# Two graph-attention layers: the second layer as (A x1) W with x1 as the stationary operand, e_i and e_j by VectorE multiply-accumulate, and its outputs in later slots

One core of one Trainium2 chip. The metric is the device time of the whole program in microseconds (us), the median over its runs; lower is better. A run is called fast when it is not over 1.5% above the fastest run of the same kernel. All runs quoted here were correct against the reference.

## The reference

128 batches of 128 nodes with 512 features, all in float32. Layer 0 is attention with 8 heads under the adjacency mask; layer 1 is a graph attention with one head. Cut to layer 1 and the frame:

```python
def _L1_gnn_ref(h, adj, W, a):
    Wh = jnp.matmul(h, W)                       # W: 512 x 512
    a1, a2 = a[:Fout, 0], a[Fout:, 0]
    e_i = jnp.einsum('bnf,f->bn', Wh, a1)
    e_j = jnp.einsum('bnf,f->bn', Wh, a2)
    e = jax.nn.leaky_relu(e_i[:, :, None] + e_j[:, None, :], negative_slope=0.2)
    e = jnp.where(adj == 0, MASK_VAL, e)
    attention = jax.nn.softmax(e, axis=2)       # A: 128 x 128 per batch
    return jax.nn.elu(jnp.matmul(attention, Wh))

x = _layernorm(x + _L0_gnn_ref(x, adj, ...))    # this is x1
x = _layernorm(x + _L1_gnn_ref(x, adj, W, a))
```

## The kernel before

Batches go in groups of four, and the loop runs over slots, one per batch. In each slot stand one batch's attention weights, a fourth of the next group's projections (slot 0: transposes of x; then pqT; pkT; pv), the attention output of the batch before, and a share of layer 1 of the group before. The Tile framework orders the instructions of each engine and picks the buffers. All small PSUM tiles come from one pool of four banks (`ps`). Layer 1 and the schedule, with cuts:

```python
def x1_transposes(g, i):                                   # 4 transposes per batch, then a VectorE copy
    transposed(X1T[g][:, :, i, :], X1[g][:, i, :], ...)

def graph_weights(g):                                      # wa = W @ a1, W @ a2
    for c in range(NC):                                    # pj: e_j on all partitions, 4 products x 512 columns
        nc.tensor.matmul(pj, wa2_bc[:, c, :], X1T[g][:, c, :, :], ...)
    for i in range(G):                                     # pi: e_i, 16 products x 1 column
        for c in range(NC):
            nc.tensor.matmul(pi[:, i:i + 1], X1T[g][:, c, i, :], wa[:, 0, c:c + 1], ...)
    ...                                                    # e, leaky relu, mask, softmax without its division

def graph_values(g):                                       # pw = x1 W: 16 products x 512 columns per group
    for i in range(G):
        for c in range(NC):
            nc.tensor.matmul(p, X1T[g][:, c, i, :], w_sb[:, c, :], ...)
        nc.scalar.copy(WH[g, i], p)

def graph_output(g, i):                                    # ph = A (x1 W): 1 product x 512 columns per batch
    nc.tensor.matmul(p, ATT_T[g][:, i, :], WH.pop((g, i)), start=True, stop=True)
    nc.scalar.activation(t, p, AF.Exp, scale=r)            # elu: ScalarE, GpSimd, VectorE in turn; p is held until y
    nc.gpsimd.tensor_scalar(t, t, 1.0, -1.0, op0=ALU.min, op1=ALU.add)
    nc.vector.scalar_tensor_tensor(y, p, r, t, op0=ALU.mult, op1=ALU.max)
    ...                                                    # + x1, layer norm, store

def layer1(g, step):
    if step == 1:   graph_weights(g); graph_values(g)
    elif step == 2: graph_weights_t(g); graph_output(g, 0); graph_output(g, 1)
    elif step == 3: graph_output(g, 2); graph_output(g, 3)
```

Of the kernel before, what the change touches and what calls it, by code (L numbers as in the profile page):

```python
# [11 lines left out]
ALU = mybir.AluOpType  # L12
AX = mybir.AxisListType

N_BATCH = 128


@with_exitstack
def tile_two_graph_layers(ctx: ExitStack, tc: tile.TileContext, x, adj, wq, bq, wk, bk, wv, bv, wo, bo, w, a, out,
                          n_batch=N_BATCH):  # L20
    """Multi-head graph attention, then single-head graph attention, each with residual and layer norm.

    A batch is 128 nodes, one partition block. Batches are taken in groups of four so that the
    projections stream 512 nodes. All matrix products are float32.
    """
    nc = tc.nc
    P = 128
    D = x.shape[2]
# [1 line left out]
    H = 8  # L30
    DH = D // H
    G = 4
    NG = n_batch // G
    NEG = -1.0e9
    EPS = 1e-5
    ALPHA = 0.2
# [6 lines left out]
    ps_big = ctx.enter_context(tc.tile_pool(name="ps_big", bufs=2, space=bass.MemoryType.PSUM))  # L43
    ps = ctx.enter_context(tc.tile_pool(name="ps", bufs=4, space=bass.MemoryType.PSUM))

    # state of the groups and batches in flight
    X, ADJ, MASK, XT, QT, KT, V, PR, X1, X1T, WH, ATT, RI, ATT_T = ({} for _ in range(14))

    def load(g):
        X[g] = three.tile([P, G, D], F32, tag="x", name=f"x_{g}")  # L50
# [4 lines left out]

    load(0)

# [1 line left out]
    ident = const.tile([P, P], F32, tag="ident", name="ident")  # L59
    make_identity(nc, ident)  # L60
    half = const.tile([P, 1], F32, tag="half", name="half")
# [24 lines left out]
    bv_bc = on_all_partitions(bv, 0, "bv")  # L86
    bo_bc = on_all_partitions(bo, 0, "bo")

    # the queries carry the 1/sqrt(head dim) of the logits
    qscale = 1.0 / DH ** 0.5  # L90
    bqs = const.tile([P, NC], F32, tag="bqs", name="bqs")
    nc.vector.tensor_scalar_mul(bqs, bq_sb, qscale)

    # W @ a1 and W @ a2, so that e_i and e_j come from the layer's input
    wa = const.tile([P, 2, NC], F32, tag="wa", name="wa")
    for s in range(2):
        a_bc = two.tile([P, D], F32, tag="o", name=f"a_bc{s}")
        nc.gpsimd.dma_start(a_bc, bass.AP(tensor=a.tensor, offset=a.offset + s * D, ap=[[0, P], [1, D]]))
        for c in range(NC):
            scr = two.tile([P, D], F32, tag="y", name=f"wa_scr{s}_{c}")  # L100
            nc.vector.scalar_tensor_tensor(scr, w_sb[:, c, :], 1.0, a_bc, op0=ALU.mult, op1=ALU.mult,
                                           accum_out=wa[:, s, c:c + 1])
    wa2_bc = const.tile([P, NC, P], F32, tag="wa2_bc", name="wa2_bc")
    nc.vector.tensor_copy(wa2_bc, wa[:, 1, :].unsqueeze(2).to_broadcast([P, NC, P]))

    def transposed(dst, src, name):
        """dst[p, c, n] = src[n, c * 128 + p]"""
        p = ps.tile([P, NC, P], F32, tag="ps", name=name)
        for c in range(NC):
            nc.tensor.transpose(p[:, c, :], src[:, c * P:(c + 1) * P], ident)  # L110
        nc.vector.tensor_copy(dst, p)  # L111
# [8 lines left out]
        nc.gpsimd.tensor_tensor(rstd, rstd, half, op=ALU.pow)  # L120
        nc.vector.tensor_scalar(dst, src, mv[:, 0:1], rstd, op0=ALU.subtract, op1=ALU.mult)  # L121

# [1 line left out]
    def x_transposes(g):  # L124
        MASK[g] = two.tile([P, G, P], I32, tag="mask", name=f"mask_{g}")
        nc.vector.tensor_scalar(MASK[g], ADJ[g], 0.0, None, op0=ALU.is_gt)
# [19 lines left out]
            nc.vector.tensor_add(V[g, i], p, bv_bc)  # L146

    def attention_weights(g, i):
        """Softmax over the unmasked keys; heads stand as (h % 2, h // 2)."""
        s = ps_big.tile([P, 2, H // 2, P], F32, tag="big", name=f"s_{g}_{i}")  # L150
        for hp in range(H // 2):
            for j in range(2):
                r = slice(j * DH, (j + 1) * DH)
                nc.tensor.matmul(s[:, j, hp, :], QT[g][r, hp, i, :], KT[g][r, hp, i, :], start=True, stop=True)  # L154
        pr = two.tile([P, H, P], F32, tag="pr", name=f"pr_{g}_{i}")
        nc.gpsimd.memset(pr, NEG)  # L156
        nc.vector.copy_predicated(pr, MASK[g][:, i, :].unsqueeze(1).to_broadcast([P, H, P]),  # L157
                                  s.rearrange("p j h k -> p (j h) k"))
        nmax = small.tile([P, H], F32, tag="nmax", name=f"nmax_{g}_{i}")
        nc.vector.tensor_reduce(nmax, pr, AX.X, ALU.max, negate=True)  # L160
        tot = small.tile([P, H], F32, tag="tot", name=f"tot_{g}_{i}")
        for h in range(H):
            nc.scalar.activation(pr[:, h, :], pr[:, h, :], AF.Exp, bias=nmax[:, h:h + 1], scale=1.0,  # L163
                                 accum_out=tot[:, h:h + 1])
        nc.vector.reciprocal(tot, tot)
        nc.gpsimd.tensor_tensor(pr, pr, tot.unsqueeze(2).to_broadcast([P, H, P]), op=ALU.mult)  # L166
        PR[g, i] = pr

    def attention_output(g, i):
        pr = PR.pop((g, i))  # L170
        pT = ps_big.tile([P, 2, H // 2, P], F32, tag="big", name=f"ppT_{g}_{i}")
        for j in range(2):
            for hp in range(H // 2):
                nc.tensor.transpose(pT[:, j, hp, :], pr[:, j * (H // 2) + hp, :], ident)  # L174
        prT = two.tile([P, 2, H // 2, P], F32, tag="prT", name=f"prT_{g}_{i}")
        nc.scalar.copy(prT, pT)  # L176
        v = V.pop((g, i))
        po = ps.tile([P, H // 2, P], F32, tag="ps", name=f"po_{g}_{i}")
        for hp in range(H // 2):
            for j in range(2):  # L180
                h = 2 * hp + j
                nc.tensor.matmul(po[j * DH:(j + 1) * DH, hp, :], v[:, h * DH:(h + 1) * DH], prT[:, j, hp, :],  # L182
                                 start=True, stop=True)
        oT = two.tile([P, H // 2, P], F32, tag="oT", name=f"oT_{g}_{i}")
        nc.scalar.copy(oT, po)  # L185
        py = ps.tile([P, D], F32, tag="ps", name=f"py_{g}_{i}")
        for c in range(NC):
            nc.tensor.matmul(py, oT[:, c, :], wo_sb[:, c, :], start=(c == 0), stop=(c == NC - 1))  # L188
        o = two.tile([P, D], F32, tag="o", name=f"o_{g}_{i}")
        nc.vector.tensor_add(o, py, bo_bc)  # L190
        nc.vector.scalar_tensor_tensor(o, o, 0.0, X[g][:, i, :], op0=ALU.max, op1=ALU.add)
        if i == 0:
            X1[g] = two.tile([P, G, D], F32, tag="x1", name=f"x1_{g}")
            X1T[g] = one.tile([P, NC, G, P], F32, tag="x1T", name=f"x1T_{g}")
        layer_norm(X1[g][:, i, :], o, f"0_{g}_{i}")

    def x1_transposes(g, i):
        transposed(X1T[g][:, :, i, :], X1[g][:, i, :], f"px1T_{g}_{i}")

# [1 line left out]
    def graph_weights(g):  # L201
        pj = ps.tile([P, G, P], F32, tag="ps", name=f"pj_{g}")
        for c in range(NC):
            nc.tensor.matmul(pj, wa2_bc[:, c, :], X1T[g][:, c, :, :], start=(c == 0), stop=(c == NC - 1))  # L204
        pi = ps.tile([P, G], F32, tag="ps", name=f"pi_{g}")
        for i in range(G):
            for c in range(NC):
                nc.tensor.matmul(pi[:, i:i + 1], X1T[g][:, c, i, :], wa[:, 0, c:c + 1],  # L208
                                 start=(c == 0), stop=(c == NC - 1))
        ei = small.tile([P, G], F32, tag="ei", name=f"ei_{g}")  # L210
        nc.vector.tensor_copy(ei, pi)
        e = one.tile([P, G, P], F32, tag="e", name=f"e_{g}")
        nc.vector.tensor_tensor(e, pj, ei.unsqueeze(2).to_broadcast([P, G, P]), op=ALU.add)
        nc.vector.scalar_tensor_tensor(e, e, ALPHA, e, op0=ALU.mult, op1=ALU.max)
        at = two.tile([P, G, P], F32, tag="at", name=f"at_{g}")
        nc.gpsimd.memset(at, NEG)
# [8 lines left out]
        nc.vector.reciprocal(RI[g], tot)  # L225
        ATT[g] = at

    def graph_values(g):
        for i in range(G):
            p = ps.tile([P, D], F32, tag="ps", name=f"pw_{g}_{i}")  # L230
            for c in range(NC):
                nc.tensor.matmul(p, X1T[g][:, c, i, :], w_sb[:, c, :], start=(c == 0), stop=(c == NC - 1))  # L232
            WH[g, i] = two.tile([P, D], F32, tag="wh", name=f"wh_{g}_{i}", bufs=4)
            nc.scalar.copy(WH[g, i], p)

    def graph_weights_t(g):
        p = ps.tile([P, G, P], F32, tag="ps", name=f"pat_{g}")
        for i in range(G):
# [1 line left out]
        ATT_T[g] = two.tile([P, G, P], F32, tag="attT", name=f"attT_{g}")  # L240
        nc.vector.tensor_copy(ATT_T[g], p)

    def graph_output(g, i):
        p = ps.tile([P, D], F32, tag="ps", name=f"ph_{g}_{i}")
        nc.tensor.matmul(p, ATT_T[g][:, i, :], WH.pop((g, i)), start=True, stop=True)  # L245
        r = RI[g][:, i:i + 1]
        # elu(h) = max(h, min(exp(h), 1) - 1), with the softmax's division in h
        t = two.tile([P, D], F32, tag="t", name=f"t_{g}_{i}")
        nc.scalar.activation(t, p, AF.Exp, scale=r)  # L249
        nc.gpsimd.tensor_scalar(t, t, 1.0, -1.0, op0=ALU.min, op1=ALU.add)  # L250
# [3 lines left out]
        layer_norm(y, y, f"1_{g}_{i}")  # L254
        nc.sync.dma_start(out[g * G + i], y)

# [1 line left out]
    # Per slot one batch's attention weights, the output of the batch before it, the layer-1 input of the batch  # L258
    # before that, and a share of the next group's projections and of the previous group's layer 1.
    def projections(g, step):  # L260
        if not 0 <= g < NG:
            return
# [11 lines left out]
    def layer1(g, step):  # L274
        if not 0 <= g < NG:
            return
        if step == 1:
            graph_weights(g)
            graph_values(g)
        elif step == 2:  # L280
            graph_weights_t(g)
            graph_output(g, 0)
            graph_output(g, 1)
        elif step == 3:
            graph_output(g, 2)
            graph_output(g, 3)

    for step in range(G):
        projections(0, step)
    slots = [(g, i) for g in range(NG) for i in range(G)]  # L290
    for t in range(len(slots) + G):
        g, i = divmod(t, G)
        if t < len(slots):
            attention_weights(g, i)
        projections(g + 1, i)
        if 0 <= t - 2 < len(slots):
            x1_transposes(*slots[t - 2])
        if 0 <= t - 1 < len(slots):
            attention_output(*slots[t - 1])
        layer1(g - 1, i)  # L300


# [22 lines left out]
```

## Time and profile before

| | before |
|---|---|
| time | 3663.18 us, median of 4 runs, 3655.35 to 3669.01 |
| TensorE busy | 3328.2 us, 91% of the span |
| VectorE, ScalarE, GpSimd busy | 36, 27, 27% |
| mean granted TensorE clock | 0.935 of full speed |
| one group of four batches | 112.6 us |

The lines are in the prediction. Two readings carry over. The group repeats 32 times, so 1 us per group is about 0.9% of the time. And the clock is part of the cost: the clock records hold only full and half, so 0.935 over 3661 us is (1 - 0.935) x 2 x 3661 = 476 us at half clock.

### The profile page before, as it was taken

The page shows a single profiled execution, that of the slowest core. Times are in us where ns is not written, and L with a number is a line of the kernel's source. Part 1 is how long each engine was busy: PE and PEld are TensorE (multiplying, and loading weights), DVE is VectorE, ACT ScalarE, POOL GpSimd, SP SyncE. Part 2 cuts the span into 40 slices and gives each one's busy share as a digit, 9 for nine tenths or more (in the row PEclk, how much of TensorE's full clock was granted, in tenths as well). Part 3 has the DMA queues.
Part 4 walks back from the last instruction along what each step waited for, and adds up shares of the span by engine and source line. Part 5 has one row for each costly group of instructions (what it writes and reads, how often), then busy time and mean ns, then how long its engine had stood idle before and what let it go on. Part 6 is the DMA issues. An engine that isn't in the chain of part 4 may idle for free.

```text
span 3661.1 us, 33875 instructions
## 1 busy us (share of the span) xinstructions
PE 3328.2 (91%) x12928; PEld 1762.8 (48%) x12928; DVE 1334.7 (36%) x2194; ACT 995.6 (27%) x3073; POOL 989.1 (27%) x1069
## 2 busy tenths in 40 slices
PE   7999999999999999999999999999999999999995
PEld 3545444455444454444544445544445444454452
DVE  2343334333343333343333433334333334333343
ACT  1222322222222223222232222222222322223231
POOL 1132223222233222232222322223322223222233
PEclk9999999999999999999999999999999999999997
DMA  3000000000000000000000000000000000000000
GB/s 112 12 26 9 20 26 26 23 12 24 21 26 24 15 21 21 26 24 26 9 21 26 27 23 12 23 21 26 24 15 21 21 26 24 26 9 20 12 12 23
DMA packets 55411, 83.98 MB, mean 23 GB/s; under 512 B 3280, under 2 KB 19664, under 8 KB 55248
## 3 DMA queue, kind: packets, MB, share of 16 engines
q1 hardware_dynamic: 52224, 75.51, 5.9%
q10 hardware_dynamic: 2640, 5.24, 0.4%
q8 instruction: 102, 1.67, 0.2%
q0 software_dynamic: 384, 1.05, 0.1%
q14 instruction: 61, 0.50, 0.0%
HBM read 48.24 MB, written 33.55 MB: 22 GB/s over the span
## 4 chain that ended last, share of the span: by engine, by line
PE 83%; POOL 6%; ACT 3%; DVE 3%; issue 3%; DMA 1%; ACTq 0%; SPq 0%; POOLq 0%; DVEq 0%
PE py L188 14%; PE pw L232 14%; PE pqT L136 12%; PE pkT L136 12%; PE pv L144 12%; PE po L182 4%; PE pj L204 3%; PE pi L208 3%; PE ppT L174 3%; POOL t L250 3%; PE ph L245 2%; POOL y L253 2%; PE px1T L110 2%; ACT prT L176 2%; PE s L154 1%
## 5 line engine op out<-in xcount | busy, mean ns | idle before, releaser
L188 PE MATMUL py<-wo,oT 128*128 128x512 f32 x1024 | 534.5, 670 | 26.6 <-ACT oT L185 23.6
L163 ACT ACTIVATE pr<-pr,nmax 128x128 f32<-128x128 f32 x1024 | 396.1, 388 | 386.4 <-DVE nmax L160 383.4
L232 PE MATMUL pw<-w,x1T 128*128 128x512 f32 x1024 | 500.9, 652 | 0.0
L111 DVE COPY x1T<-px1T 128x512 f32<-128x512 f32 x128 | 87.8, 686 | 1049.8 <-PE px1T L110 1049.6
L156 POOL MEMSET pr<- 128x1024 f32 x128 | 121.8, 952 | 1269.4 <-PE ppT L174 1269.4
L136 PE MATMUL pqT<-xT,wq 128*128 128x512 f32 x1024 | 446.4, 594 | 16.3 <-DVE xT L111 16.3
L136 PE MATMUL pkT<-xT,wk 128*128 128x512 f32 x1024 | 444.8, 592 | 0.0
L144 PE MATMUL pv<-wv,xT 128*128 128x512 f32 x1024 | 444.7, 592 | 0.0
L166 POOL TENSOR_TENSOR pr<-pr,tot 128x1024 f32<-128x1024 f32 x128 | 243.6, 1903 | 454.4 <-DVE mv L118 245.2
L232 PEld LDWEIGHTS pw<-w,x1T 128*128 128x128 f32 x1024 | 210.9, 209 | 264.4 <-issue 264.4
L188 PEld LDWEIGHTS py<-wo,oT 128*128 128x128 f32 x1024 | 208.1, 214 | 267.9 <-issue 220.8
L250 POOL TENSOR_SCALAR t<-t 128x512 f32<-128x512 f32 x128 | 247.6, 1943 | 326.1 <-ACT t L249 323.6
L136 PEld LDWEIGHTS pqT<-xT,wq 128*128 128x128 f32 x1024 | 195.0, 191 | 261.8 <-issue 244.8
L144 PEld LDWEIGHTS pv<-wv,xT 128*128 128x128 f32 x1024 | 194.6, 190 | 244.9 <-issue 237.7
L136 PEld LDWEIGHTS pkT<-xT,wk 128*128 128x128 f32 x1024 | 194.5, 190 | 244.6 <-issue 244.2
L157 DVE COPY_PREDICATED pr<-mask,s 128x1024 f32<-128x1024 int32 x128 | 169.4, 1323 | 213.4 <-PE s L154 213.4
L185 ACT COPY oT<-po 128x512 f32<-128x512 f32 x128 | 75.0, 586 | 628.0 <-PE po L182 628.0
L121 DVE TENSOR_SCALAR x<-o,mv,rstd 128x512 f32<-128x512 f32 x128 | 97.0, 758 | 329.7 <-POOL rstd L120 329.7
L154 PE MATMUL s<-kT,qT 64*128 64x128 f32 x2048 | 211.4, 300 | 2.4 <-DVE pr L157 2.4
L190 DVE TENSOR_TENSOR o<-py,bo 128x512 f32<-128x512 f32 x128 | 88.5, 692 | 324.7 <-PE py L188 324.7
L110 PE MATMUL pxT<-ident,x 128*128 128x128 f32 x512 | 77.2, 287 | 140.2 <-DVE y L252 130.5
L138 ACT ACTIVATE qT<-pqT,bqs 128x512 f32<-128x512 f32 x128 | 88.0, 687 | 386.2 <-PE pqT L136 386.2
(62 smaller groups left out, 3547.9 us busy)
## 6 DMA issues: line engine op xcount, KB each, us to landing
x<-in_x_dram SPq DMA_DIRECT2D x32, 1024.0 KB, 5.3
out_dram<-y SPq DMA_DIRECT2D x128, 256.0 KB, 2.0
adj<-in_adj_dram SPq DMA_DIRECT2D x32, 256.0 KB, 2.8
wq<-in_L_gnn_Wq_dram ACTq DMA_DIRECT2D x1, 1024.0 KB, 10.8
wk<-in_L_gnn_Wk_dram ACTq DMA_DIRECT2D x1, 1024.0 KB, 16.3
wv<-in_L_gnn_Wv_dram ACTq DMA_DIRECT2D x1, 1024.0 KB, 20.7
wo<-in_L_gnn_Wo_dram ACTq DMA_DIRECT2D x1, 1024.0 KB, 15.0
w<-in_L_gnn_W_dram ACTq DMA_DIRECT2D x1, 1024.0 KB, 14.0
```

Source lines behind the costliest of these rows:

```text
L110: nc.tensor.transpose(p[:, c, :], src[:, c * P:(c + 1) * P], ident)
L136: nc.tensor.matmul(p, w_t[:, c, f * P:(f + 1) * P], XT[g][:, c, :, :], start=(c == 0), stop=(c == NC - 1))
L144: nc.tensor.matmul(p, XT[g][:, c, i, :], wv_sb[:, c, :], start=(c == 0), stop=(c == NC - 1))
L154: nc.tensor.matmul(s[:, j, hp, :], QT[g][r, hp, i, :], KT[g][r, hp, i, :], start=True, stop=True)
L156: nc.gpsimd.memset(pr, NEG)
L157: nc.vector.copy_predicated(pr, MASK[g][:, i, :].unsqueeze(1).to_broadcast([P, H, P]), s.rearrange("p j h k -> p (j h) k"))
L163: nc.scalar.activation(pr[:, h, :], pr[:, h, :], AF.Exp, bias=nmax[:, h:h + 1], scale=1.0, accum_out=tot[:, h:h + 1])
L166: nc.gpsimd.tensor_tensor(pr, pr, tot.unsqueeze(2).to_broadcast([P, H, P]), op=ALU.mult)
L182: nc.tensor.matmul(po[j * DH:(j + 1) * DH, hp, :], v[:, h * DH:(h + 1) * DH], prT[:, j, hp, :], start=True, stop=True)
L188: nc.tensor.matmul(py, oT[:, c, :], wo_sb[:, c, :], start=(c == 0), stop=(c == NC - 1))
L232: nc.tensor.matmul(p, X1T[g][:, c, i, :], w_sb[:, c, :], start=(c == 0), stop=(c == NC - 1))
L250: nc.gpsimd.tensor_scalar(t, t, 1.0, -1.0, op0=ALU.min, op1=ALU.add)
```

## The change

The intent: since A (x1 W) = (A x1) W, and TensorE takes its stationary operand untransposed, (A x1) transposed comes out of a product with x1 as it lies. x1 need not be transposed if e_i and e_j come from elsewhere: two VectorE multiply-accumulates per batch against W a1 and W a2, broadcast to all partitions. The diff, cut to its core:

```diff
@@ preamble
+    wa_bc = const.tile([P, 2, D], F32, tag="wa_bc", name="wa_bc")
+    for s in range(2):
+        for c in range(NC):
+            nc.tensor.transpose(p[:, c, :], wa[:, s, c:c + 1].to_broadcast([P, P]), ident)
+        nc.vector.tensor_copy(wa_bc[:, s, :], p.rearrange("p c k -> p (c k)"))
@@ attention_output, after x1's layer norm
+        for s, e in enumerate((EI, EJ)):
+            nc.vector.scalar_tensor_tensor(scr, x1, 1.0, wa_bc[:, s, :], op0=ALU.mult, op1=ALU.mult,
+                                           accum_out=e[g][:, i:i + 1])
-    def x1_transposes(g, i): ...
@@ graph_weights
-        for c in range(NC):
-            nc.tensor.matmul(pj, wa2_bc[:, c, :], X1T[g][:, c, :, :], ...)
-        ...                                                # pi, 16 products
+        for i in range(G):
+            nc.tensor.transpose(pj[:, i, :], EJ[g][:, i:i + 1].to_broadcast([P, P]), ident)
-    def graph_values(g): ...
+    def graph_mix(g, i):
+        for c in range(NC):
+            nc.tensor.matmul(p[:, c, :], X1[g][:, i, c * P:(c + 1) * P], ATT_T[g][:, i, :], start=True, stop=True)
+        nc.scalar.copy(ZT[g, i], p)
@@ graph_output
-        nc.tensor.matmul(p, ATT_T[g][:, i, :], WH.pop((g, i)), start=True, stop=True)
+        for c in range(NC):
+            nc.tensor.matmul(p, zT[:, c, :], w_sb[:, c, :], start=(c == 0), stop=(c == NC - 1))
@@ layer1
-        step 1: graph_weights, graph_values    step 2: weights_t, output 0, 1    step 3: output 2, 3
+        step 1: graph_weights                  step 2: weights_t, mix 0, 1, output 0
+        step 3: mix 2, 3, output 1             step 4 (slot 0 of the next group): output 2, 3
```

More of the change, by code (lines that the diff above doesn't have):

```diff
@@ L13, with tile_two_graph_layers @@
 AX = mybir.AxisListType
-N_BATCH = 128
 @with_exitstack
-def tile_two_graph_layers(ctx: ExitStack, tc: tile.TileContext, x, adj, wq, bq, wk, bk, wv, bv, wo, bo, w, a, out,
-                          n_batch=N_BATCH):
+def tile_two_graph_layers(ctx: ExitStack, tc: tile.TileContext, x, adj, wq, bq, wk, bk, wv, bv, wo, bo, w, a, out):
     nc = tc.nc
@@ L32, in tile_two_graph_layers @@
     G = 4
-    NG = n_batch // G
+    NG = x.shape[0] // G
     NEG = -1.0e9
@@ L44, in tile_two_graph_layers @@
     ps = ctx.enter_context(tc.tile_pool(name="ps", bufs=4, space=bass.MemoryType.PSUM))
-    X, ADJ, MASK, XT, QT, KT, V, PR, X1, X1T, WH, ATT, RI, ATT_T = ({} for _ in range(14))
+    X, ADJ, MASK, XT, QT, KT, V, PR, X1, EI, EJ, ATT, RI, ATT_T, ZT = ({} for _ in range(15))
     def load(g):
@@ L102, in tile_two_graph_layers @@
                                            accum_out=wa[:, s, c:c + 1])
-    wa2_bc = const.tile([P, NC, P], F32, tag="wa2_bc", name="wa2_bc")
-    nc.vector.tensor_copy(wa2_bc, wa[:, 1, :].unsqueeze(2).to_broadcast([P, NC, P]))
+    wa_bc = const.tile([P, 2, D], F32, tag="wa_bc", name="wa_bc")
+    for s in range(2):
+        p = ps.tile([P, NC, P], F32, tag="ps", name=f"pwa{s}")
+        for c in range(NC):
+            nc.tensor.transpose(p[:, c, :], wa[:, s, c:c + 1].to_broadcast([P, P]), ident)
+        nc.vector.tensor_copy(wa_bc[:, s, :], p.rearrange("p c k -> p (c k)"))
     def transposed(dst, src, name):
@@ L193, in attention_output @@
             X1[g] = two.tile([P, G, D], F32, tag="x1", name=f"x1_{g}")
-            X1T[g] = one.tile([P, NC, G, P], F32, tag="x1T", name=f"x1T_{g}")
-        layer_norm(X1[g][:, i, :], o, f"0_{g}_{i}")
-    def x1_transposes(g, i):
-        transposed(X1T[g][:, :, i, :], X1[g][:, i, :], f"px1T_{g}_{i}")
+            EI[g] = small.tile([P, G], F32, tag="ei", name=f"ei_{g}")
+            EJ[g] = small.tile([P, G], F32, tag="ej", name=f"ej_{g}")
+        x1 = X1[g][:, i, :]
+        layer_norm(x1, o, f"0_{g}_{i}")
+        for s, e in enumerate((EI, EJ)):
+            scr = two.tile([P, D], F32, tag="scr", name=f"scr{s}_{g}_{i}")
+            nc.vector.scalar_tensor_tensor(scr, x1, 1.0, wa_bc[:, s, :], op0=ALU.mult, op1=ALU.mult,
+                                           accum_out=e[g][:, i:i + 1])
     def graph_weights(g):
         pj = ps.tile([P, G, P], F32, tag="ps", name=f"pj_{g}")
-        for c in range(NC):
-            nc.tensor.matmul(pj, wa2_bc[:, c, :], X1T[g][:, c, :, :], start=(c == 0), stop=(c == NC - 1))
-        pi = ps.tile([P, G], F32, tag="ps", name=f"pi_{g}")
         for i in range(G):
-            for c in range(NC):
-                nc.tensor.matmul(pi[:, i:i + 1], X1T[g][:, c, i, :], wa[:, 0, c:c + 1],
-                                 start=(c == 0), stop=(c == NC - 1))
-        ei = small.tile([P, G], F32, tag="ei", name=f"ei_{g}")
-        nc.vector.tensor_copy(ei, pi)
+            nc.tensor.transpose(pj[:, i, :], EJ[g][:, i:i + 1].to_broadcast([P, P]), ident)
         e = one.tile([P, G, P], F32, tag="e", name=f"e_{g}")
-        nc.vector.tensor_tensor(e, pj, ei.unsqueeze(2).to_broadcast([P, G, P]), op=ALU.add)
+        nc.vector.tensor_tensor(e, pj, EI[g].unsqueeze(2).to_broadcast([P, G, P]), op=ALU.add)
         nc.vector.scalar_tensor_tensor(e, e, ALPHA, e, op0=ALU.mult, op1=ALU.max)
@@ L226, in graph_weights @@
         ATT[g] = at
-    def graph_values(g):
-        for i in range(G):
-            p = ps.tile([P, D], F32, tag="ps", name=f"pw_{g}_{i}")
-            for c in range(NC):
-                nc.tensor.matmul(p, X1T[g][:, c, i, :], w_sb[:, c, :], start=(c == 0), stop=(c == NC - 1))
-            WH[g, i] = two.tile([P, D], F32, tag="wh", name=f"wh_{g}_{i}", bufs=4)
-            nc.scalar.copy(WH[g, i], p)
     def graph_weights_t(g):
@@ L241, in graph_weights_t @@
         nc.vector.tensor_copy(ATT_T[g], p)
+    def graph_mix(g, i):
+        p = ps.tile([P, NC, P], F32, tag="ps", name=f"pz_{g}_{i}")
+        for c in range(NC):
+            nc.tensor.matmul(p[:, c, :], X1[g][:, i, c * P:(c + 1) * P], ATT_T[g][:, i, :], start=True, stop=True)
+        ZT[g, i] = two.tile([P, NC, P], F32, tag="zT", name=f"zT_{g}_{i}")
+        nc.scalar.copy(ZT[g, i], p)
     def graph_output(g, i):
         p = ps.tile([P, D], F32, tag="ps", name=f"ph_{g}_{i}")
-        nc.tensor.matmul(p, ATT_T[g][:, i, :], WH.pop((g, i)), start=True, stop=True)
+        zT = ZT.pop((g, i))
+        for c in range(NC):
+            nc.tensor.matmul(p, zT[:, c, :], w_sb[:, c, :], start=(c == 0), stop=(c == NC - 1))
         r = RI[g][:, i:i + 1]
@@ L278, in layer1 @@
             graph_weights(g)
-            graph_values(g)
         elif step == 2:
             graph_weights_t(g)
+            graph_mix(g, 0)
+            graph_mix(g, 1)
             graph_output(g, 0)
+        elif step == 3:
+            graph_mix(g, 2)
+            graph_mix(g, 3)
             graph_output(g, 1)
-        elif step == 3:
+        elif step == 4:
             graph_output(g, 2)
@@ L290, in tile_two_graph_layers @@
     slots = [(g, i) for g in range(NG) for i in range(G)]
-    for t in range(len(slots) + G):
+    for t in range(len(slots) + G + 1):
         g, i = divmod(t, G)
@@ L295, in tile_two_graph_layers @@
         projections(g + 1, i)
-        if 0 <= t - 2 < len(slots):
-            x1_transposes(*slots[t - 2])
         if 0 <= t - 1 < len(slots):
@@ L300, in tile_two_graph_layers @@
         layer1(g - 1, i)
+        if i == 0:
+            layer1(g - 2, 4)
 _INS = ["x", "adj", "L0_gnn_Wq", "L0_gnn_bq", "L0_gnn_Wk", "L0_gnn_bk", "L0_gnn_Wv", "L0_gnn_bv", "L0_gnn_Wo",
```

## The prediction

> **What bounds the kernel now.** I read the profile page first, then the timeline of TensorE over one group of four batches, then the waits of TensorE, then the groups of instructions, then the busy time and clock by stretch. On the page, the engines' busy times and the chain of work that ended last:
>
> ```profile
> PE 3328.2 (91%) x12928; PEld 1762.8 (48%) x12928; DVE 1334.7 (36%) x2194; ACT 995.6 (27%) x3073; POOL 989.1 (27%) x1069
> ...
> PE 83%; POOL 6%; ACT 3%; DVE 3%; issue 3%; DMA 1%; ACTq 0%; SPq 0%; POOLq 0%; DVEq 0%
> ```
>
> TensorE is the bound: 91% busy and 83% of the chain, with DMA at 1%. What counts is the time between starts on TensorE, so I take that from its timeline. The group between 1801.37 and 1914.00 us repeats 112.63 us later, and so do the groups before it; its lines that the change touches, and its stalls:
>
> ```profile
> 1825.68 0.65 PE L110 MATMUL pxT<-ident,x 128*128 128x128 f32 x4 [1.14 <-DVE y L252]
> ...
> 1831.43 0.66 PE L110 MATMUL pxT<-ident,x 128*128 128x128 f32 x4 [3.35 <-DVE y L252]
> ...
> 1835.39 1.12 PE L110 MATMUL px1T<-ident,x 128*128 128x128 f32 x4 [2.89 <-DVE xT L111]
> ...
> 1839.16 5.73 PE L188 MATMUL py<-wo,oT 128*128 128x512 f32 x8 [0.74 <-ACT oT L185]
> ...
> 1862.92 3.70 PE L188 MATMUL py<-wo,oT 128*128 128x512 f32 x8
> 1866.46 3.60 PE L204 MATMUL pj<-x1T,wa_bc 128*128 128x512 f32 x8
> 1869.89 3.63 PE L208 MATMUL pi<-wa,x1T 128*128 128x1 f32 x32
> 1873.38 15.68 PE L232 MATMUL pw<-w,x1T 128*128 128x512 f32 x32
> 1888.90 13.90 PE L136 MATMUL pkT<-xT,wk 128*128 128x512 f32 x32
> 1902.63 0.60 PE L110 MATMUL px1T<-ident,x 128*128 128x128 f32 x4
> ```
>
> The second number is the duration, the bracket the idle time before and its releaser. Three things are seen. A product over 512 columns makes two records, and 32 of them (pkT) take 13.73 us from start to start, 0.43 us each. The 32 records of pi, which stream one column each, still take 3.49 us, 0.11 us each: the weight loads set that. And once per group TensorE idles 1.14+3.35+2.89+0.74 = 8.12 us, and the py after it takes 5.73 us where the others take 3.70. The waits of TensorE say that this is nearly all the waiting there is:
>
> ```profile
> PE pxT L110 <- DVE y L252: 130.5, 58, 3.4
> PE px1T L110 <- DVE xT L111: 83.9, 29, 2.9
> PE py L188 <- ACT oT L185: 23.6, 32, 1.0
> ```
>
> The x transposes need PSUM buffers that the two last layer-1 outputs hold until VectorE's y, which itself waits for GpSimd's t (1.94 us each, two in a row). The clock by stretch (the column before the DMA share) explains the slow py and the slow pw:
>
> ```profile
> 1833.00:1843.30 10.30, 7.16 (x25) 4.14 (x26) 7.27 (x12) 4.99 (x26) 3.24 (x4) 0.50 0.14 53
> 1843.30:1874.30 31.00, 30.70 (x131) 17.22 (x130) 9.73 (x17) 9.11 (x31) 6.27 (x7) 1.00 0.11 35
> 1874.30:1877.70 3.40, 3.40 (x5) 1.29 (x4) 2.26 (x4) 1.00 (x5) 0.00 (x0) 0.54 0.15 44
> ```
>
> The clock is halved for about 10.2 us after the stalls and for 3.4 us after pi, inside pw.
>
> **What the Trainium skill says.** (1) "FP8 and Floating Point Precision", section TensorE Precision Notes: true FP32 takes 4 passes through the array. The trace agrees: two records of 0.429 us for 512 columns are 4 x 512 columns at 2.4 per ns. So a product costs its moving columns times four. (2) "TensorE: Matmul & The Clock Gate", section LDWEIGHTS (loading the stationary operand): about P/1.2 ns for P columns, here 107 ns; pi shows 0.109 us per record. Loads are said to run ahead under matmuls (section Step-by-step), and pkT's 0.429 leaves no room for a load beside it. (3) Same page, What's actually happening: the clock is either full or half, judged over free-running windows of 3413 ns. The trace agrees: the dips are about 3 and 1 such windows, and 112.63 us is 33.0 of them, so the period seems locked to the window. (4) "SBUF — State Buffer", section Who interferes with whom: VectorE and GpSimd share one port pair, as a lock. GpSimd's t is 1.927 to 1.949 us in all 128 cases, so it shows nothing there; VectorE's x normalisation, 0.55 us alone and 1.15 us at 1828.98 beside GpSimd, does.
>
> **The change, part by part** (per group of four batches, time between starts on TensorE).
> Removed: px1T 16 transposes x 0.11 = 1.8; pj 3.4; pi 3.5; pw 15.5; ph, four products of two records, 8 x 0.43 to 0.45 = 3.6. Sum 27.8.
> Added: pj as four transposes, 0.4. pz, 16 products with 128 moving columns: 32 records, load 107 ns, streaming 2 x 128 columns also 107 ns; if one hides under the other, as in s (six records in 0.64 us), 32 x 0.108 = 3.5. ph, now 16 products over 512 columns: 32 x 0.43 = 13.8. Sum 17.7. The streamed columns of the layer's two products are the same in both orders (before 4 x 512 + 512, after 4 x 128 + 4 x 512 per batch); the saving is in the transposes, pj, pi, and in the halved clock after pi (1.8 of pw's 15.5).
> Net -10.1 us of work at full clock.
>
> VectorE: two multiply-accumulates per batch, 0.69 + 0.08 us as the eight of the preamble show, against one 0.69 us copy of x1T: +3.4 us per group, about +3% of the span, off the path. ScalarE: a copy of zT for a copy of wh, equal.
>
> The waits move too, since the third and fourth layer-1 outputs now follow the x transposes. From the order of instructions per engine I lay out the critical stretch by hand with the durations above, from the end of pv = 0: po 1.05; s, py to 5.4; pz 2 and 3 to 7.1; ph 1 to 10.6; s to 10.8; three pxT and six transposes ppT to 12.75. The fourth pxT needs ph 1's buffer: ScalarE copies zT 3 (to 11.3), exp (to 11.9), GpSimd t 1.94 (to 13.9), VectorE y (to 14.65). TensorE waits 1.95. Then pxT, ppT, s, po, s to 18.25. py needs oT, which stands on ScalarE behind eight exps (3.1 us in all), which wait for nmax, which stands on VectorE behind that y: nmax to 15.8, prT to 16.5, exps to 19.6, oT to 20.2. TensorE waits 2.0. So 8.1 us of stall become about 4.
>
> Sum for the period at full clock: slot 3 of a group 10.8; slot 0, 19.9 with both stalls; slot 1 (pqT 13.73, attention 7.5, pj 0.4, pkT 13.73) 35.4; slot 2 (attention 9.3, pz 1.7, ph 3.5, pv 13.7) 28.3. Together 94.4 us, against 112.6. (Check: 112.6 - 10.1 - 4.1 and the 3.6 us that the halved clock costs outside pw gives 94.8.) I keep 1.5 us for a halved clock in the stall, partial or in some groups: the stretch from 10.8 to 20.2 has 4 us idle and much of the rest transposes. Period 96.
>
> Around it: before, about 30 such periods are 3379 us, and 282 us are preamble, first group and tail. The preamble grows: the transposes of wa stand first on TensorE and their copies ahead of xT on VectorE, and W lands at 31.6 us with its eight products ending at 36.6; pqT starts at about 40.4 instead of 27.7, +12.7. The tail shrinks by some 24: the last layer 1 no longer runs px1T, pj, pi, pw (27 us from x1 to pat's end and on) before its first output, though four ph of 3.5 us follow. 282 + 13 - 24 = 271. Total 30 x 96 + 271 = 3151 us.
>
> **Rivals.**
> A: *the loads of pz are not hidden.* Each record then costs 107 + 107 ns, +3.4 us per group, 32 groups: 3260 us. For it: s uses half the rows, so its 0.107 may rest on two halves working at once. Against: under pkT the loads vanish with all rows in use. One in six.
> B: *the stall stays or moves.* Two PSUM-holding chains through GpSimd still exist, and the clock halves for three windows again (before, a stall of 8 us cost 3.6 more). Then 8 us of stall, 94.4 + 4 + 3.5 = 102: 3330 us. For it: oT behind exps. Against: only one ph stands before the transposes. One in eight.
> C: *VectorE's extra 6 us per group or the port shared with GpSimd delays y or nmax and so TensorE.* VectorE would be 48% busy at the new span, and in my layout is free from 11.0 before pr; the cost is 1 us per group at most: +30.
> D: *no halved clock at all*: period 94.4 or, with shorter waits, 92: 3030 to 3100 us.
> A gain under 2% would need +13 us per group over my sum; only A and B together come near, so I give it little.
>
> **Range and chances.** Centre 3150; D reaches down to 3060, A up to 3260; B lies just outside. Range 3060 to 3275. Chances: faster 0.97, same 0.02, slower 0.01.
>
> **What would show it.** Right: TensorE's pi and px1T gone; pz 0.11 us per record from start to start; ph 0.43; the period of the timeline 94 to 97 us; the wait of pxT for y about 2 us per group and py for oT about 2; the granted clock above 0.96; no half clock between pj and pkT; VectorE near 1450 us busy. Wrong: pz at 0.2 us per record (A); waits of TensorE over 200 us in sum with the clock under 0.94 (B); a new wait of ph for zT or of pz for attT over 1 us per group; a period locked at 99 us, 29 windows.

## The result, and the profile after

| | before | after |
|---|---|---|
| time, median (range) of 4 runs | 3663.18 (3655.35 to 3669.01) | 3166.01 (3163.89 to 3166.32) |
| ratio to before | | 0.8645, 95% interval 0.8628 to 0.8662 |
| TensorE busy | 91% | 94% |
| VectorE busy | 1334.7 us | 1464.0 us |
| mean granted clock | 0.935 | 0.972 |

A ratio is the mean time of one kernel's fast runs over that of the other's of the same rounds, so not quite the ratio of the medians. All runs here were fast. The page of the kernel after, busy times and the chain that ended last:

```profile
PE 2976.5 (94%) x12040; PEld 1580.0 (50%) x12040; DVE 1464.0 (46%) x2547; ACT 989.1 (31%) x3073; POOL 994.9 (31%) x1069
...
PE 80%; DVE 6%; POOL 6%; issue 4%; ACT 3%; DMA 1%; POOLq 0%; ACTq 0%; DVEq 0%
```

TensorE is still the bound. Its timeline over one group of the kernel after, the lines that answer to those of before (start, duration, what, and in brackets the idle time before it):

```profile
1728.17 0.60 PE L211 MATMUL pj<-ident,ej 128*128 128x128 f32 x4
1728.61 13.90 PE L137 MATMUL pkT<-xT,wk 128*128 128x512 f32 x32
...
1751.45 2.05 PE L238 MATMUL pz<-attT,x 128*128 128x128 f32 x16
1753.43 0.49 PE L155 MATMUL s<-kT,qT 64*128 64x128 f32 x4
1753.86 3.70 PE L246 MATMUL ph<-w,zT 128*128 128x512 f32 x8
1757.39 13.90 PE L145 MATMUL pv<-wv,xT 128*128 128x512 f32 x32
...
1776.59 1.95 PE L238 MATMUL pz<-attT,x 128*128 128x128 f32 x16
1778.38 3.60 PE L246 MATMUL ph<-w,zT 128*128 128x512 f32 x8
...
1784.41 0.66 PE L111 MATMUL pxT<-ident,x 128*128 128x128 f32 x4
...
1787.41 0.71 PE L155 MATMUL s<-kT,qT 64*128 64x128 f32 x6
1790.99 5.40 PE L189 MATMUL py<-wo,oT 128*128 128x512 f32 x8 [2.87 <-DVE xT L112]
1796.22 7.03 PE L246 MATMUL ph<-w,zT 128*128 128x512 f32 x16
1803.09 13.90 PE L137 MATMUL pqT<-xT,wq 128*128 128x512 f32 x32
```

From start to start: pj is now 0.44 us; the 32 records of pz take 1.98 (with one short wait) and 1.79 us, so 0.11 us a record; ph takes 3.53 + 3.53 + 6.87 = 13.9 us. px1T, pi and pw are gone. pxT (the fourth x transpose, at 1784.41) no longer waits. One long stall is left, 2.87 us before py, and that py still takes 5.23 us where the others take 3.54. The waits of TensorE in the kernel after:

```profile
PE py L189 <- DVE xT L112: 80.4, 28, 3.0
PE pwa L104 <- DVE wa_scr L97: 32.0, 1, 32.0
PE po L183 <- ACT prT L177: 29.0, 96, 4.1
```

Two of these need care. The first is put down to VectorE's copy xT, as the event that came last, but py itself waits on ScalarE's oT: in the built program, which lists for each instruction the semaphores that it waits for, py has one wait, and it is on ScalarE's. In the next group oT and py are seen to follow each other, in ScalarE's and TensorE's timelines of the kernel after:

```profile
1886.15 0.39 ACT L164 ACTIVATE pr<-pr,nmax 128x128 f32<-128x128 f32 x1
1886.54 0.56 ACT L186 COPY oT<-po 128x512 f32<-128x512 f32 x1
```

```profile
1887.15 5.17 PE L189 MATMUL py<-wo,oT 128*128 128x512 f32 x8 [2.87 <-DVE xT L112]
```

oT ends at 1887.10, and it stands on ScalarE directly behind the eight exps. xT's copy ended at 1887.13, so the order of the two alone decides nothing; the wait in the program does. The second wait, 32 us, is the preamble: the transposes of wa stand first on TensorE.

The clock by stretch in the kernel after (before the DMA share):

```profile
1878.00:1887.10 9.10, 6.05 (x59) 4.99 (x58) 7.06 (x13) 5.84 (x20) 4.90 (x5) 0.98 0.01 2
1887.10:1890.50 3.40, 3.35 (x5) 1.56 (x6) 2.52 (x4) 0.78 (x4) 1.90 (x1) 0.55 0.20 77
1890.50:1899.00 8.50, 8.50 (x21) 3.74 (x20) 3.81 (x7) 3.09 (x15) 4.15 (x4) 1.00 0.33 123
```

One half-clock stretch of 3.4 us is left here, on py. In the trace's clock records the dips (stretches at half clock) of the kernel after come 28 windows of 3.413 us apart, every third or fourth time 29, with the dip before each longer step lasting two windows; over 29 of them the mean distance is 96.5 us. That mean is the period. The kernel before has its dips 21 and 12 windows apart in turn, 33 together. Dips begin on window edges, so their distances are whole windows; a group need not be. From pv to the next pv, steady groups of the kernel after take 95.9 to 97.8 us, 28.1 to 28.6 windows.

### The profile page after: what moved, and what is told of

Its sections match the earlier page's. It is cut to its first block, busy times and chain, and to the rows that moved or that the text cites. A ratio compares the mean times of both kernels' runs of the same rounds, so it can differ in the third digit from the quotient of the medians.

```text
span 3164.1 us, 32460 instructions
## 1 busy us (share of the span) xinstructions
PE 2976.5 (94%) x12040; PEld 1580.0 (50%) x12040; DVE 1464.0 (46%) x2547; ACT 989.1 (31%) x3073; POOL 994.9 (31%) x1069
## 4 chain that ended last, share of the span: by engine, by line
PE 80%; DVE 6%; POOL 6%; issue 4%; ACT 3%; DMA 1%; POOLq 0%; ACTq 0%; DVEq 0%
PE py L189 17%; PE pqT L137 14%; PE pkT L137 14%; PE pv L145 14%; PE ph L246 10%; PE po L183 3%; PE ppT L175 3%; POOL t L251 2%; PE pz L238 2%; PE s L155 2%; ACT prT L177 2%; POOL y L254 2%; DVE st L118 1%; DVE xT L112 1%; POOL rstd L121 1%
## 5 line engine op out<-in xcount | busy, mean ns | idle before, releaser
L246 PE MATMUL ph<-w,zT 128*128 128x512 f32 x1024 | 459.1, 596 | 0.0
L120 POOL TENSOR_SCALAR rstd<-mv 128x1 f32<-128x1 f32 x256 | 56.8, 222 | 881.3 <-DVE mv L119 588.5
L246 PEld LDWEIGHTS ph<-w,zT 128*128 128x128 f32 x1024 | 189.9, 190 | 220.4 <-issue 216.8
L122 DVE TENSOR_SCALAR x<-o,mv,rstd 128x512 f32<-128x512 f32 x128 | 129.8, 1014 | 213.3 <-POOL rstd L121 213.3
L155 PE MATMUL s<-kT,qT 64*128 64x128 f32 x2048 | 224.8, 300 | 3.8 <-DVE pr L158 3.8
L155 PEld LDWEIGHTS s<-kT,qT 64*128 64x128 f32 x2048 | 164.8, 186 | 73.8 <-issue 65.9
```

Of the source, the lines that this page charges most:

```text
L122: nc.vector.tensor_scalar(dst, src, mv[:, 0:1], rstd, op0=ALU.subtract, op1=ALU.mult)
L155: nc.tensor.matmul(s[:, j, hp, :], QT[g][r, hp, i, :], KT[g][r, hp, i, :], start=True, stop=True)
L246: nc.tensor.matmul(p, zT[:, c, :], w_sb[:, c, :], start=(c == 0), stop=(c == NC - 1))
```

## The experiments

My theory after the result: the saving is TensorE work (pi, pj, px1T) plus a shorter stall, and the stall got shorter because two layer-1 outputs moved away from the x transposes. Its rivals: that the order of the products is itself the gain; that the schedule counts for nothing; and that the clock dips belong to something else than stalls and pi. The first four runs take the change apart.

### 1. Only the scores by VectorE

```diff
 # the kernel before, with
+ wa_bc, EI, EJ and the two multiply-accumulates, pj as four transposes
- pi, pj as products
  # px1T, pw, ph and the old schedule kept; at, attT and scr single-buffered, so that SBUF holds it
```

> The kernel before with only the scores changed: e_i and e_j by VectorE, pj as four transposes, px1T, pw, ph and the old schedule kept (at, attT and scr single-buffered so that SBUF holds it). My theory: TensorE loses pj 3.4 - 0.4 us and pi 3.5 us per group and the halved clock in pw (1.8 us) goes, 8.3 us of 112.6; the stall of 8.1 us and its halved clock stay. Preamble +12.5 us. Period near 104, total 3663 - 31 x 8.3 + 12.5 = 3418 us, pw 13.7 to 13.9 us per group. Rival (the clock dip in pw belongs to pw, not to pi): pw stays at 15.5 and the total is near 3474 us. Second rival (the stall was mostly filled by chance and grows when the layer-1 chain comes 7 us earlier): over 3500 us.

Measured: 3457.69 us, ratio 0.9437 (0.9421 to 0.9452), clock 0.934. The period went from 33 to 31 windows (105.8 us). TensorE's timeline:

```profile
1854.65 1.12 PE L114 MATMUL px1T<-ident,x 128*128 128x128 f32 x4 [3.27 <-DVE xT L115]
...
1886.34 0.60 PE L215 MATMUL pj<-ident,ej 128*128 128x128 f32 x4
1886.78 13.90 PE L236 MATMUL pw<-w,x1T 128*128 128x512 f32 x32
1900.52 13.90 PE L140 MATMUL pkT<-xT,wk 128*128 128x512 f32 x32
```

pw takes 13.74 us from start to start without pi ahead of it, against 15.52: the dip in pw goes with pi (runs 9 and 10 show when). The saving is 40 us short of my 8.3 us per group because the stall did not stay at 8.1 us: its waits are 1.14 + 3.81 + 3.27 + 0.54 + 0.73 = 9.5 us in this group, and four windows run at half clock instead of three behind it. The second rival is right in direction, not in size. The single buffers are a second difference of this run, and no run tells what they cost.

### 2. Only the order of the products

```diff
 # the kernel before, with
- graph_values; ph = A (x1 W)
+ graph_mix (pz); ph = (A x1) W
  # px1T, pi and pj kept; outputs 0, 1 in step 2, mixes and outputs 2, 3 in step 3
```

> The kernel before with only the order of the products changed: (A x1) W, with px1T, pj and pi kept for the scores and the old schedule. My theory: pw 15.5 and ph 3.6 us per group go, pz 3.6 and ph 13.8 come; the halved clock after pi then falls on pkT, +1.8. Net 0 us per group, total 3620 to 3700 us. Rival (the order itself is the gain, since the stationary operand needs no transposed x1): under 3500 us.

Measured: 3518.84 us, ratio 0.9607 (0.9590 to 0.9624), clock 0.954. My theory, net 0, is wrong, and the rival is right that there is a gain, though not by its reason: px1T is still there. TensorE's waits say where it comes from:

```profile
PE s L154 <- DVE pr L157: 88.3, 31, 3.7
PE po L182 <- ACT prT L176: 16.1, 63, 1.1
```

The waits of pxT for y and of px1T for xT, 130.5 and 83.9 us before, are gone; one wait of about 2.9 us per group took their place. The clock is 0.954 in place of 0.935, 323 us at half clock in place of 476. Before, the two ph ahead of the x transposes were 0.9 us each, and GpSimd's two t of 1.94 us came in one block behind them. Now each ph is 3.5 us of TensorE work, so the first output's exp, t and y run under the second output. The same work of TensorE is better spread: this step of my sum compared work with work and left out what work does for the waits.

### 3. Only the schedule

```diff
 # the kernel before, with
-        step 2: outputs 0, 1     step 3: outputs 2, 3
+        step 2: output 0         step 3: output 1      step 4 (slot 0 of the next group): outputs 2, 3
```

> The kernel before with only the layer-1 outputs moved: output 1 in the last slot, outputs 2 and 3 in the first slot of the next group. My theory: one output instead of two before the x transposes, so the stall falls from 8.1 us to 3 to 4 us per group and the halved clock from three windows to one or two: 5 to 7 us per group, total 3450 to 3520 us. Rival (the stall only moves to another wait, or the period stays locked at 33 windows): 3640 to 3680 us.

Measured: 3533.03 us, ratio 0.9641 (0.9626 to 0.9656), clock 0.942. The wait of pxT for y is down to 0.21 us in the group looked at, but px1T still waits 2.26 for xT and py 0.74 for oT, and py is still at half clock (5.23 us from start to start). That is 13 us beyond the slow end of what I expected; the "only moves" rival falls.

### 4. The changed kernel with the old schedule

```diff
 # the kernel after, with
-        step 2: mix 0, 1, output 0    step 3: mix 2, 3, output 1         step 4: outputs 2, 3
+        step 2: mix 0, 1, outputs 0, 1    step 3: mix 2, 3, outputs 2, 3
```

> The changed kernel with the old schedule: mixes 2 and 3 and outputs 2 and 3 in the last slot, two outputs before the x transposes. My theory: the stall of 8 us and three half-clock windows come back, +5 to 7 us per group: 3320 to 3390 us. Rival (the gain is all in the removed TensorE work, the schedule is neutral): 3150 to 3180 us.

Measured: 3237.44 us, ratio 0.8836 (0.8822 to 0.8850), clock 0.952. Neither: the schedule is worth 71 us of the 3237, not 150 to 220 and not nothing. The 8 us stall does not come back:

```profile
PE s L155 <- DVE pr L158: 88.1, 31, 4.2
```

In the timeline, py has the other wait:

```profile
1842.81 3.70 PE L189 MATMUL py<-wo,oT 128*128 128x512 f32 x8 [0.69 <-ACT oT L186]
```

2.87 us per group at s and 0.69 at py stand against 2.87 at py in the kernel after, so the waits differ by little. The clock differs: 0.952 and 0.972 make 311 and 177 us at half clock, and 134 us more of it can cost up to half, 67 of the 71 us.

Taken alone, the three parts save 209, 148 and 133 us, 490 in sum, and together 497 (with the kernel before 3 us faster). That looks additive and is not: moving the outputs saves 133 us from the kernel before and 71 us from the kernel that has the other two, since the order of the products and the schedule shorten the same stall. The other way round, scores and order together (run 4) save 429 us where they save 209 + 148 = 357 alone. One reason is in the code: px1T can go only when both are in, and it took 2.46 us per group, some 76 us in 31 groups. The two differences, -62 and +72 us, happen to cancel.

### 5. An output ahead of the py that waits

If py's stall is oT behind the exps, work that needs neither should fill it. Layer-1 output 2 goes ahead of the attention output in slot 0:

```diff
         projections(g + 1, i)
+        if i == 0:
+            layer1(g - 2, 4)          # output 2
         if 0 <= t - 1 < len(slots):
             attention_output(*slots[t - 1])
         layer1(g - 1, i)
         if i == 0:
-            layer1(g - 2, 4)          # outputs 2, 3
+            layer1(g - 2, 5)          # output 3
```

> The changed kernel with layer-1 output 2 issued ahead of the attention output of the first slot, so that 3.5 us of products stand between the x transposes and the py that waits for oT. My theory (py waits 2.9 us for ScalarE's oT behind eight exps, and the idle stretch halves the clock for one or two windows): the wait falls under 1 us, the halved windows go, 4.5 us per group: 3020 to 3060 us, clock above 0.99. Rival (the wait moves behind the filler because the exps wait for nmax behind y, and the clock still dips): 3130 to 3170 us.

Measured: 3044.99 us, ratio 0.8310 (0.8296 to 0.8324), clock 0.994. TensorE's timeline:

```profile
1813.74 3.70 PE L246 MATMUL ph<-w,zT 128*128 128x512 f32 x8 [0.81 <-DVE y L253]
1817.38 1.09 PE L183 MATMUL po<-prT,v 128*64 128x128 f32 x16
1818.40 0.72 PE L155 MATMUL s<-kT,qT 64*128 64x128 f32 x8
1819.19 3.70 PE L189 MATMUL py<-wo,oT 128*128 128x512 f32 x8
```

The wait became 0.81 us for y, py takes 3.54, and from the first steady group to the tail the trace has no half-clock window. py starts 92.4 us after the py of the same slot in the group before (1800.69 to 1893.13, both for the py ahead of pz). That is 4.1 us less than the mean of the kernel after: 2.06 us are the shorter wait, and its 4.4 us of half clock per group, which can cost up to half, are gone.

### 6. W's products after the first projections

```diff
-    wa, wa_bc = ...                     # before anything on TensorE
     for step in range(G):
         projections(0, step)
+    wa, wa_bc = ...
```

> The changed kernel with the eight products of W and a and their transposes put after the first group's projections. My theory: the first pqT no longer waits for W, 12 to 13 us off the preamble: 3153 us. Rival (the preamble is hidden or the work lands on the path later): 3166 us, no change.

Measured: 3153.66 us, ratio 0.8608 (0.8595 to 0.8621). In medians 12.4 us less than the kernel after. It was run at another time. By the ratios to before, 0.8608 and 0.8645, the difference is 0.0037 x 3663 = 13.6 us.

### 7. Both

```diff
 # the kernel after, with the edits of 5 and 6
```

> Both of these at once. If they are independent the savings add: 3005 to 3050 us, faster than either kernel. If the steady part reacts to the shifted start (phase of the clock windows), the sum is off by up to 30 us.

Measured: 3033.44 us (3032.62 to 3034.77, 4 runs), ratio 0.8280 (0.8268 to 0.8293), clock 0.994. It beats both kernels: by 17% the one before and, 0.8280 over 0.8645, by 4.2% the one after. The savings add: 11.6 us below run 5.

### 8. The multiply-accumulates twice

```diff
-        for s, e in enumerate((EI, EJ)):
+        for s, e in ((0, EI), (1, EJ), (0, EI), (1, EJ)):
```

> The changed kernel with the two multiply-accumulates per batch done twice (the same result written again): 6.2 us more VectorE work per group. My theory: off the path, VectorE goes from 46 to 52% busy and the time stays within 0.5%, 3150 to 3182 us. Rival (they delay nmax, exps and oT in the first slot): the wait of py grows by up to 1.5 us per group and the time by 30 to 100 us.

Measured: 3161.09 us, ratio 0.8630 (0.8616 to 0.8644) against 0.8645: the same. VectorE rose from 46 to 51% busy. About 0.7 us of the wait moved from py to pxT:

```profile
PE py L189 <- DVE xT L112: 59.9, 28, 2.4
...
PE pxT L111 <- DVE xT L112: 18.7, 29, 0.7
```

The cost of e_i and e_j on VectorE is off the path, as predicted.

### 9 and 10. A little more work for TensorE

The period of the kernel before is 33.0 clock windows in every steady group. Is it held there? Extra transposes that write the same result again, in a stretch at full clock:

```diff
-        for i in range(G):
+        for i in 2 * list(range(G)):      # run 9; run 10: 5 * list(range(G))
             nc.tensor.transpose(p[:, i, :], ATT[g][:, i, :], ident)
```

> The kernel before with the four transposes of the attention weights done twice per group, 0.44 us more of TensorE work in a stretch at full clock. Lock theory (the group's period is held at 33 clock windows, 112.64 us, because a later restart leaves less work in the halved window): the period stays at exactly 33.0 windows, the halved py gets shorter, and the time changes by under 5 us. Rival (33 is a coincidence): +0.44 x 31 = +14 us and the dips no longer come at constant distance.

> The same with the four transposes done five times, 1.76 us more per group. Lock theory: the halved py holds about 4 us of work at half clock, a loss of 2 us, so 1.76 us nearly uses up what the lock can absorb: either still 33 windows and under 10 us, or a mix of 33 and 34 windows, +20 to +110 us in whole windows. Rival: +1.76 x 31 = +55 us with a period of 114.4 us, 33.5 windows, in every group alike.

Measured: with 0.44 us more per group, 3628.11 us, ratio 0.9913 (0.9895 to 0.9931), 0.9% **faster** (clear of 1, and no run of the one overlaps the other's); with 1.76 us more, 3669.27 us, ratio 1.0019 (1.0004 to 1.0034), where plain addition gives +55 us, 1.5%. The timeline of the first, in a group of 32 windows:

```profile
1822.71 1.11 PE L110 MATMUL px1T<-ident,x 128*128 128x128 f32 x4 [2.73 <-DVE xT L111]
1823.76 1.98 PE L182 MATMUL po<-prT,v 128*64 128x128 f32 x16
1826.47 3.70 PE L188 MATMUL py<-wo,oT 128*128 128x512 f32 x8 [0.74 <-ACT oT L185]
...
1858.67 13.98 PE L232 MATMUL pw<-w,x1T 128*128 128x512 f32 x32
```

px1T and po are still at half clock, but py is not (3.54 us from start to start against 5.57), and pw behind pi is not either. The stalls are nearly those of before (1.29, 3.13, 2.73, 0.74). So most of the gain is the clock: 0.950 against 0.935 is 362 us at half clock instead of 476, 114 us less; at up to half a microsecond lost per one, that is up to 57 us, and 34 us of gain on top of 14 us of added work need 48. Both my lock at 33 windows and its rival, plain addition, fall.

What stands is where pi falls. Five runs have pi (the kernel before, runs 2, 3, 9 and 10), 160 groups in all. In 127 of them a stretch at half clock begins within 5 us of pi's start: all those where pi starts up to 1.2 us after a window edge, or 1.94 us and more. In the other 33 none does, and they are all those where pi starts 1.29 to 1.91 us after an edge, so that its 3.49 us are split between two windows and neither holds much over 2 us of it. 31 of 32 groups of the kernel before have this dip, 18 of run 9 and 21 of run 10. Whole windows are no rule for the period: from pv to pv the steady groups take 33.0 windows in the kernel before and 31.0 in run 1, but 32.1 to 33.2 in run 9 and 32.4 to 33.7 in run 10. Why those two kernels settle on whole windows and the others do not is not shown.

## Why the prediction was right

Forecast 3150 us, range 3060 to 3275; measured 3166.

- **The sum of work** held: -10.1 us per group. From start to start, px1T 2.46 (part of it at half clock), pj 3.43, pi 3.49, pw 15.52 and ph 3.62 went, 28.5 us; pj 0.44, pz 3.77 and ph 13.9 came, 18.1 us. Net -10.4.
- **The hidden loads** held: 0.11 us per record of pz, so rival A, which needed 0.2, falls.
- **VectorE off the path** held: run 8. Its x normalisation did grow from 758 to 1014 ns in the mean. In both kernels it takes 0.55 us in the 67 cases in which GpSimd runs nothing beside it; beside a GpSimd instruction it took up to 1.47 us before and up to 2.11 us after. So running beside GpSimd costs something, but off the path (rival C). That rival's "48% busy" left out the copies of x1T that go; 46% was measured.
- **The preamble** held: pqT starts at 40.18 us; 40.4 was forecast. Run 6 measures 12 to 14 us, 12.7 was forecast. Preamble, first group and tail come to 3164 - 30 x 96.5 = 269 us, 271 was forecast.
- **The stalls** were half wrong in kind and 1.1 us too large in sum: 1.95 us at pxT and 2.0 at py were forecast, none and 2.87 measured. The failed step is "The fourth pxT needs ph 1's buffer". I took the four PSUM buffers in strict turn. In the built program the fourth pxT waits for VectorE's copy of the first pxT, whose bank it gets. TensorE therefore runs ahead and meets the one wait that is left, oT behind the exps behind nmax behind y, in full. That chain was forecast rightly.
- **The cause of the shorter stall** was only half seen. I put it to "the third and fourth layer-1 outputs now follow the x transposes". Run 4 shows that without that move the stalls are 3.6 us per group, not 8: the 3.5 us ph products space the outputs by themselves.
- **The clock** was allowed 1.5 us per group and took about 1.7 on py. The mean period is 96.5 us, 96 was forecast; the difference in total, 15 us, is this. That it is so near is in part luck. By the timeline of one group, the stretch from the end of pv to pqT takes 31.9 us (30.7 and 1.5 for the clock were forecast), pqT to the end of pkT 35.4 (35.4) and from there to the end of pv 28.9 (28.3): the shorter stall made good much of the short waits and two-window dips that the sum left out. Rival D was not how the kernel came, but it is what run 5 makes of it: no half clock, a period of 92.4 us where I had written 92, and 3045 us inside its 3030 to 3100.

## What to carry to other kernels

Where TensorE is the bound, sum the work from start to start, and then ask of each product what waits run under it: a long product between two others can be worth more than its cost. When a stall is left, look in the program for the wait on the instruction itself, since the event that came last in the trace may be another, and fill it with work that needs none of that chain. A saving or a loss of a microsecond per iteration can be undone or turned round by the clock, so read the granted clock beside every time.

## What the Trainium skill lacked or had wrong

- "TensorE: Matmul & The Clock Gate" ties the halved clock to idle gaps. Here half clock also followed 32 back-to-back records of one column each (pi, 3.49 us, no idle between in the profile): pw took 15.52 us behind pi and 13.74 without it (run 1). It did so in 127 of 160 groups, and in none where pi started 1.29 to 1.91 us after a window edge.
- The same page, Back-to-back issue gap, gives about 131 ns per sustained matmul of 512 columns and about 216 ns for an isolated one. Here 32 records take 13.73 us; at the two passes per record that "FP8 and Floating Point Precision" implies, that is an estimated 214.5 ns a pass in a sustained stream: the figure called isolated (which the page elsewhere gives as the back-to-back gap too; it names no type for the 131).
- No page says that in a repeating kernel added work can pay through the clock: 0.44 us more per group made it 0.9% faster, with a clock of 0.950 in place of 0.935, and 1.76 us cost 0.2% in place of 1.5% (runs 9 and 10).
